# RWKV6 in a hybrid block on one core: layernorm statistics from ScalarE's sums in two passes, the decay's mixed token added by TensorE and multiplied by VectorE

## The chip, the core and the metric

The kernel runs on one core of a Trainium2 chip. A core has five engines, each with its own in-order instruction queue: TensorE (PE; its weight loads are listed as PEld), VectorE (DVE), ScalarE (ACT), GpSimd (POOL) and SyncE (SP), which only issues DMAs. TensorE reads SBUF and writes PSUM; ScalarE and VectorE read both; GpSimd works in SBUF only here. The metric is the device time of one execution in microseconds (us); 0.3% of it is about what can be told from no change.

## The reference

Four layers with residual sums, each on a layernorm of its input: a retention (attention) layer, a mixture of experts (MoE: 8 experts, the best 2 per token), the RWKV6 layer, and the same MoE again. There are 4 sequences of 1024 tokens with 256 channels, all float32.

```python
def _layernorm(x, axis=-1, eps=1e-05):
    m = jnp.mean(x, axis=axis, keepdims=True)
    v = jnp.var(x, axis=axis, keepdims=True)
    return (x - m) / jnp.sqrt(v + eps)
...
x = x + attention(_layernorm(x))
x = x + moe(_layernorm(x))
x = x + rwkv6(_layernorm(x))
x = x + moe(_layernorm(x))
```

What RWKV6 computes, as far as the change touches it:

```python
sx = shifted(x) - x
m = jnp.tanh((x + sx * time_maa_x) @ tm_w1).reshape(Bb, Tt, 5, A)
mix = time_maa_wkvrg + jnp.einsum('btfa,fac->btfc', m, tm_w2)
xw, xk, xv, xr, xg = [x + sx * mix[:, :, i] for i in range(5)]
r, k, v, g = xr @ Wr, xk @ Wk, xv @ Wv, silu(xg @ Wg)
w = jnp.exp(-jnp.exp(time_decay + jnp.tanh(xw @ td_w1) @ td_w2))
# per head, for each token: y = r (state + u k v); state = w state + k v
```

After that y is normalized per head, multiplied by g and by Wo, and added to x. The "decay's mixed token" is xw, the first of the five.

## The kernel before

**Tiling.** The 4096 tokens are eight blocks of 512 (two to a sequence); a block's residual `res[j]` stays in SBUF as 128 tokens x 4 tiles x 256 channels. RWKV works on it transposed: 128 channels by 512 tokens, two channel groups g. The stages follow one another: retention, first MoE, RWKV, second MoE.

**The RWKV stage** is written out by hand. `step(j, n, ...)` (L1272) is step n of block j, eight steps to a block; a step has two halves h. `run(j, n, h)` (L1088) does one part of the recurrence: VectorE multiplies k into the spread-out v (L1094) and runs two scans of 512 tokens (L1096), then GpSimd multiplies by r (L1104). TensorE sums the result into w_yp (L1127). Other work is put between the runs by tables: `given` (L1211) makes the mixed tokens of block j+1, `amid` (L1220) stands in the middle of a step, `late` (L1230) at its end, `uses` (L1240) between the two scans of a run. Through these, block j's recurrence goes on beside the output of block j-1, the projections of block j+1 and the layernorm of block j+2.

**Who decides the order.** TensorE and ScalarE run in program order through the whole kernel, VectorE and GpSimd from the first MoE on, SP in the RWKV stage. What is written later in the program waits behind what is written earlier on the same engine, whether it needs it or not. The products that RWKV makes in PSUM take three banks with the tag "mm" in turn: w_mp, w_dp, w_cp, w_pp, w_yc, w_twp, w_rp and others. A product waits until the bank that was used three products earlier has been read.

**What the change touches.**
- `stats_of` (L201): for each of the four tiles of a block, `bn_stats` and `bn_aggr` on VectorE (L206, L207) give mean and variance; GpSimd forms rstd by `inv_sqrt` (L198, L199) and shift = -mean rstd (L209, L210).
- `normed` of RWKV (L911), at step 5 of block j for block j+2: `stats_of`, then four ScalarE ACTIVATEs that scale and shift (L919), then the token before the block (L923 or L925).
- `Piece.block` (L484) and `Piece.tokens` (L500, by L495): the same for the router of the second MoE, for one finished block n at a time: statistics at the end of step 7 of block n+1, the normalized tokens at the end of step 0 of block n+2, their transposes (`turned`) in step 2, the logits at the end of step 3 (L1543 to L1549).
- `deltas` (L954): a mixed token in two channel groups. TensorE makes w_dp (L964), ScalarE adds `maa` while it reads PSUM (L976), GpSimd multiplies by sx and adds the token (L977, L978). For the tokens 0 and 2 of blocks 6 and 7 one VectorE instruction takes the place of L976 and L977:

```python
                    if f in (0, 2) and j >= NBLK - 2:
                        nc.vector.scalar_tensor_tensor(xf, dp, maa, sx, ALU.add, ALU.mult)
                    else:
                        nc.scalar.activation(xf, dp, AF.Identity, bias=maa)
                        nc.gpsimd.tensor_mul(xf, xf, sx)
                    nc.gpsimd.tensor_add(xf, xf, d["now"][:, c, :])
```

- `decay` (L982), in the middle of step 4 for block j+1: w_twp (L986) is the decay's mixed token times td_w1, and ScalarE's tanh reads it (L989).

**Near them, in one block.** Step 0: `factors(1)` gives the second half of w_wk (L1036, L1037), which `paired` (w_rk, L1019) reads; `mix` makes w_m (L947 to L952), which w_dp needs. Step 1: w_dp of tokens 2 and 0 for the first channel group, `own` (w_cp, L1025), the projection g with Silu (w_gT, L1011, with a table load on ScalarE), `centre` (w_yc, L1140), and the second w_cp; `bonus` (L1030) on VectorE reads w_cp. Step 2: w_dp of tokens 2 and 0 for the second group. Steps 3 and 4: tokens 1 and 3, `root` (L1163 to L1167), `gated` (L1181 to L1183: w_cen, w_sq). Steps 6 and 7: w_op (L225), the projections k and r (L1013), the first half of w_wk for the next block. Block 0 has no block ahead of it: `prepare` (L1268) makes its mixed tokens and its w_twp during the last tiles of the first MoE.

Of the kernel before, what the change touches and what calls it, by code (L numbers as in the profile page):

```python
# [39 lines left out]
F32 = mybir.dt.float32  # L40
I32 = mybir.dt.int32
AF = mybir.ActivationFunctionType
ALU = mybir.AluOpType
AX = mybir.AxisListType

P = 128
B, T, C = 4, 1024, 256
KC = C // P
BLK = 512
NB = T // BLK  # L50
NT = BLK // P
H, D = 16, 16
GH = P // D
E = 8
# [4 lines left out]
NBLK = B * NB  # L59
# [3 lines left out]
HB = NBLK // 2  # L63
HT = HB * NT
# [44 lines left out]
def hybrid_kernel(  # L109
# [24 lines left out]
    nc = tc.nc  # L134
    mm = nc.tensor.matmul
# [3 lines left out]
    def pool(name, side="left"):  # L139
        return tc.alloc_tile_pool(name=name, bufs=1, side=side, reuse_waits="tile")  # L140
# [5 lines left out]
    small = tc.alloc_tile_pool(name="small", bufs=4)  # L146
    ps = banks("ps")

    def psum(shape, name, tag="mm"):

        t = ps.tile([P, 512], F32, name=name, tag=tag, bufs=3 if tag == "mm" else 1)
        n = int(np.prod(shape[1:]))
        if len(shape) == 2:
            return t[:, :n]
        return t[:, :n].rearrange("p (a b) -> p a b", b=shape[2])
# [4 lines left out]
    res = {}  # L160
# [34 lines left out]
    def inv_sqrt(o, var, n, name, scale=1.0):  # L195

        t = small.tile([P, n], F32, name=name, tag=f"var{n}", bufs=2)
        nc.gpsimd.tensor_scalar(t, var, scale, EPS, ALU.mult, ALU.add)  # L198
        nc.gpsimd.tensor_tensor(o, t, mhalf[:, :n], ALU.pow)  # L199

    def stats_of(r, rstd, shift, who):  # L201

        mv = small.tile([P, NT, 2], F32, name=f"{who}mv", tag="mv")
        for i in range(NT):
            st = small.tile([P, 6], F32, name=f"{who}st", tag="st")
            nc.vector.bn_stats(st, r[:, i, :])  # L206
            nc.vector.bn_aggr(mv[:, i, :], st)  # L207
        inv_sqrt(rstd, mv[:, :, 1], NT, f"{who}ve")
        nc.gpsimd.tensor_scalar(shift, mv[:, :, 0], -1.0, None, ALU.mult)  # L209
        nc.gpsimd.tensor_tensor(shift, shift, rstd, ALU.mult)  # L210

    def across(xn, n, out, who):

        tp = psum([P, 2 * KC, P], f"{who}xtp").rearrange("p (i k) t -> p i k t", k=KC)
        for i in range(2):
            for k in range(KC):
                nc.tensor.transpose(tp[:, i, k, :], xn(2 * n + i)[:, k * P : (k + 1) * P], ident)
        nc.scalar.copy(out.rearrange("p k (i t) -> p i k t", i=2), tp)
# [251 lines left out]
    class Piece:  # L470
# [6 lines left out]
        def sm(self, shape, name, dt=F32, bufs=1):  # L477
# [3 lines left out]
            t = t[:, : int(np.prod(shape))]  # L481
            return t if len(shape) == 1 else t.rearrange("p (a b) -> p a b", b=shape[1])

        def block(self, n):  # L484

            if n == 0:
                self.logit = self.sm([HT, E], "m_logit")
                self.rstd = self.sm([HT], "m_rstd", bufs=2)
                self.shift = self.sm([HT], "m_shift", bufs=2)
            cols = slice(n * NT, (n + 1) * NT)  # L490
            stats_of(res[self.start + n], self.rstd[:, cols], self.shift[:, cols], "m_")

        def normed(self, xn, i):

            nc.scalar.activation(  # L495
                xn, res[self.start + i // NT][:, i % NT, :], AF.Identity,
                scale=self.rstd[:, i : i + 1], bias=self.shift[:, i : i + 1],
            )

        def tokens(self, n):  # L500
            xn = self.xn = [ph.tile([P, C], F32, name="m_xn", tag="m_xn", bufs=4) for i in range(NT)]
            for i in range(NT):
                self.normed(xn[i], n * NT + i)

        def turned(self):
            tT = self.tT = ph.tile([P, KC, BLK], F32, name="m_tT", tag="m_tT", bufs=1)
# [389 lines left out]
    def rwkv(pi, w):  # L896
# [3 lines left out]
        st = [dict() for _ in range(NBLK)]  # L900
# [3 lines left out]
        def half(where, name, bufs=2):  # L904
            return where.tile([P, BLK], F32, name=name, tag=name, bufs=bufs)

        def full(where, name, bufs=2, n=BLK):
            return where.tile([P, KC, n], F32, name=name, tag=name, bufs=bufs)


        def normed(j):  # L911
            d = st[j]
            r = res[j]
            rstd = small.tile([P, NT], F32, name="w_rstd", tag="rstd")
            shift = small.tile([P, NT], F32, name="w_shift", tag="shift")
            stats_of(r, rstd, shift, "w_")
            xn = d["xn"] = pi.tile([P, NT, C], F32, name="w_xn", tag="w_xn", bufs=1)
            for i in range(NT):
                nc.scalar.activation(xn[:, i, :], r[:, i, :], AF.Identity,  # L919
                                     scale=rstd[:, i : i + 1], bias=shift[:, i : i + 1])  # L920
            xT = d["xT"] = full(pi, "w_xT", n=BLK + 1)
            if j % NB == 0:
                nc.gpsimd.memset(xT[:, :, 0:1], 0.0)  # L923
            else:
                nc.gpsimd.tensor_copy(xT[:, :, 0:1], st[j - 1]["xT"][:, :, BLK : BLK + 1])  # L925
# [28 lines left out]
        def deltas(j, parts):  # L954


            d = st[j]
            dps = []

            def product(f, c):  # L960
                rows = slice(32 * f, 32 * f + 32) if f < 4 else slice(0, 32)
                wt, m = (w["tm_w2a"], d["m", 0]) if f < 4 else (w["tm_w2b"], d["m", 1])
                dp = psum([P, BLK], "w_dp")
                mm(dp, lhsT=wt[rows, c * P : (c + 1) * P], rhs=m[rows, :], start=True, stop=True)  # L964
                dps.append((f, c, dp))

            def mixed():
                for f, c, dp in dps:
                    if c == 0:
                        d["xf", f] = full(pi, "w_xf", 4)  # L970
                    xf = d["xf", f][:, c, :]
                    maa, sx = vec[:, c, V_MAA + f : V_MAA + f + 1], d["sx"][:, c, :]
                    if f in (0, 2) and j >= NBLK - 2:
                        nc.vector.scalar_tensor_tensor(xf, dp, maa, sx, ALU.add, ALU.mult)
                    else:
                        nc.scalar.activation(xf, dp, AF.Identity, bias=maa)  # L976
                        nc.gpsimd.tensor_mul(xf, xf, sx)  # L977
                    nc.gpsimd.tensor_add(xf, xf, d["now"][:, c, :])  # L978

            return [lambda f=f, c=c: product(f, c) for f, c in parts], mixed  # L980

        def decay(j):  # L982
            d = st[j]
            tp = psum([P, BLK], "w_twp")
            for c in range(KC):
                mm(tp[:64, :], lhsT=w["td_w1"][:, c, :], rhs=d["xf", 0][:, c, :],  # L986
                   start=(c == 0), stop=(c == KC - 1))
            d["tw"] = half(pi, "w_tw", 1)
            nc.scalar.activation(d["tw"][:64, :], tp[:64, :], AF.Tanh)  # L989

# [200 lines left out]
        def both(j, parts):  # L1191
# [4 lines left out]

        first = [
            [(0, normed)],
            [(0, turn)],
            [(0, mix, 0), (0, mix, 1)],  # L1200
            [(0, both, [(0, 0), (0, 1)])],
            [(0, both, [(1, 0), (1, 1)])],
            [(0, both, [(2, 0), (2, 1)]), (0, decay), (1, normed)],
            [(0, both, [(3, 0), (3, 1)])],
            [],
# [17 lines left out]
            2: [(1, mix, 1)],  # L1223
            3: [(1, projected, "v", 2)],
            4: [(-1, spread_out, 0), (1, decay)],
            5: [(1, decay2), (2, normed)],
            6: [(1, projected, "k", 1)],
            7: [(-1, out_part, 2), (1, projected, "r", 3), (1, factors, 0)],
        }
        late = {  # L1230
# [1 line left out]
            1: [(-1, centre, 1), (0, own, 1)],  # L1232
            2: [(-1, spread)],
            3: [],
            4: [(-1, spread_out, 1)],
            5: [(1, store)],
            6: [(-1, out_part, 0)],
            7: [(2, turn), (0, centre, 0)],
# [150 lines left out]
    bias = keep.tile([P, E], F32, name="bias")  # L1389
    nc.sync.dma_start(out=bias, in_=router_b.partition_broadcast(P))  # L1390
    ph = pool("ph")
# [46 lines left out]
    m, mid = moes[0].pieces[:2]  # L1438
# [38 lines left out]
    extra, made = {}, {}  # L1477

    def add(j, f, *a):
        extra.setdefault(j, []).append((f, *a))  # L1480
# [20 lines left out]
    def inputs():  # L1501
        prt.release()
        pi = made["pi"] = pool("pi")
        made["w"] = rwkv_inputs(pi)
        made["rwkv"] = rwkv(pi, made["w"])
# [13 lines left out]
    pi, w = made["pi"], made["w"]  # L1519
# [17 lines left out]
    extra, mids, fronts = {}, {}, {}  # L1537
# [4 lines left out]
        add(SENT[i], next_a.send, i)  # L1542
    for n in range(2 * HB - 1):  # L1543
        m = [p for p in moe.pieces if p.start <= n][-1]
        add(8 * n + 15, m.block, n - m.start)
        add(8 * n + 16, m.tokens, n - m.start)
        fronts[8 * n + 18] = [(m.turned,)]
        add(8 * n + 19, m.product)
        mids[8 * n + 20] = [(m.biased, n - m.start)]  # L1549
# [157 lines left out]
```

## Time and profile before

| | us |
|---|---|
| median of 5 runs | 1609.4 |
| lowest, highest | 1605.38, 1614.41 |
| the profiled execution | 1611.12 |
| its span | 1609.3 |
| busy in the span: PE, PEld | 1359.9, 713.4 |
| busy in the span: DVE, ACT, POOL | 1017.0, 603.6, 924.6 |

The profile is one execution, taken by the hardware profiler, with a span from its first to its last instruction. The page cuts the span into 40 equal slices and gives for each engine the busy share of a slice in tenths (9 is 90% or more). A group is all instructions of one line, operation and shape; behind it stand the busy time, the mean duration of one in ns, and the idle time of the engine just ahead of them with what ended it. In a timeline each line gives start, length, engine, line, operation, output <- inputs and shapes, and in brackets the idle time before it and who ended that. Names such as w_dp are the program's tiles. TensorE's matmuls of float32 data are recorded in parts, so counts on PE are higher than in the program. "Clock" is the share of full speed that TensorE was granted.

The groups that the change counts, in the whole span: L206 and L207 for m_ and w_ together 96 and 96 instructions, L977 72, L978 80, L974 8.

### The profile page before, as it was taken

The numbers are of one execution on the slowest core, as the hardware profiler recorded it, in microseconds if no ns is written. First come the engines' busy times: TensorE is split into PE (matmuls) and PEld (weight loads), VectorE is DVE, ScalarE is ACT, GpSimd is POOL, SyncE is SP. The second block draws the span as 40 slices with busy tenths as digits, with TensorE's granted clock in tenths as the row PEclk, the third lists the DMA queues.
The fourth block names the chain that finished last, engine by engine and source line by source line (L and its number), as shares of the span: only waits on it lengthen the run. The fifth ranks groups of instructions, "written<-read, shape, count | busy, mean of one in ns | idle before, by whom it ended". The sixth has DMA issues, their size and how long they took to land.

```text
span 1609.3 us, 21021 instructions
## 1 busy us (share of the span) xinstructions
PE 1359.9 (84%) x6652; PEld 713.4 (44%) x6652; DVE 1017.0 (63%) x2004; ACT 603.6 (38%) x1436; POOL 924.6 (57%) x881
## 2 busy tenths in 40 slices
PE   5999998868889988987879797887697577889993
PEld 3666665545545644422233232332232234456562
DVE  6566557424433343297988888999989962523444
ACT  2343434333433334434334444443244324333331
POOL 4233323633553326399989898987599844453331
PEclk9999999968889999998879798997789788899997
DMA  8991111131323341256656454534346832232545
GB/s 292 335 316 51 54 54 53 63 114 54 124 93 96 120 130 60 63 143 153 165 128 156 117 141 108 151 101 113 89 126 166 249 124 76 89 106 93 185 131 180
DMA packets 117548, 207.70 MB, mean 129 GB/s; under 512 B 12193, under 2 KB 80001, under 8 KB 117441
## 3 DMA queue, kind: packets, MB, share of 16 engines
q1 hardware_dynamic: 95904, 160.20, 34.5%
q0 software_dynamic: 17184, 39.86, 8.0%
q10 hardware_dynamic: 4352, 6.29, 1.3%
q8 instruction: 57, 0.93, 0.3%
q14 instruction: 51, 0.41, 0.1%
HBM read 139.18 MB, written 67.14 MB: 128 GB/s over the span
## 4 chain that ended last, share of the span: by engine, by line
PE 53%; DVE 17%; POOL 12%; ACT 6%; issue 6%; DMA 4%; another core or an unknown queue 1%; SPq 0%; ACTq 0%; POOLq 0%; DVEq 0%
PE m_hp L788 13%; PE m_op L825 6%; DVE w_s L1096 5%; POOL w_s L1104 5%; PE w_pp L1008 4%; PE a_qkp L291 3%; PE w_yp L1127 2%; PE a_yp L350 2%; DVE w_vb L1094 2%; PE w_dp L964 2%; PE m_lp L520 2%; PE a_sp L330 2%; PE m_xtp L781 2%; PE a_gp L273 2%; PE a_op L225 2%
## 5 line engine op out<-in xcount | busy, mean ns | idle before, releaser
L1104 POOL TENSOR_TENSOR w_s<-w_s,w_rT 128x1024 f32<-128x1024 f32 x128 | 304.1, 2415 | 34.3 <-DVE w_s L1096 30.6
L831 POOL DMA_INDIRECT y_all<-m_y,m_to x142 | 137.3, 967 | 305.0 <-ACT m_xt L783 173.4
L788 PE MATMUL m_hp<-w1a,m_xt 128*128 x568 | 289.1, 634 | 17.4 <-ACT m_xt L783 11.8
L794 DVE TENSOR_TENSOR m_a<-m_hp,m_sg 128x256 f32<-128x256 f32 x142 | 60.1, 424 | 292.7 <-ACT m_sg L792 268.4
L1094 DVE TENSOR_TENSOR w_vb<-w_vb,w_wk 128x1024 f32<-128x1024 f32 x128 | 153.4, 1199 | 28.3 <-ACT w_wk L1037 26.6
L1096 DVE TENSOR_TENSOR_SCAN w_s<-w_wk,w_carry,w_vb 128x512 f32<-128x512 f32 x128 | 161.0, 1276 | 9.3 <-PE w_yp L1127 1.1
L825 PE MATMUL m_op<-w2a,m_aT 128*128 x568 | 152.3, 392 | 13.3 <-ACT m_y L830 7.1
L1096 DVE TENSOR_TENSOR_SCAN w_s<-w_wk,w_vb 128x512 f32<-128x512 f32 x128 | 152.8, 1216 | 15.5 <-ACT w_carry L1114 7.1
L737 POOL DMA_INDIRECT xg_all<-m_row,m_at x128 | 125.5, 980 | 47.6 <-issue 31.3
L788 PEld LDWEIGHTS m_hp<-w1a,m_xt 128*128 128x128 f32 x568 | 103.6, 203 | 94.7 <-issue 80.2
L1127 PE MATMUL w_yp<-w_s,core_c 128*32 128x512 f32 x512 | 100.1, 688 | 44.5 <-POOL w_s L1104 33.2
L792 ACT ACTIVATE m_sg<-m_hp 128x256 f32<-128x256 f32 x142 | 54.5, 384 | 168.3 <-PE m_hp L788 150.8
L830 ACT ACTIVATE m_y<-m_op,m_share 128x256 f32<-128x256 f32 x142 | 67.2, 473 | 128.9 <-PE m_op L825 103.6
L303 POOL TENSOR_TENSOR a_t<-a_t,a_t 128x512 f32<-128x512 f32 x32 | 41.1, 1284 | 123.7 <-DVE a_t L302 104.4
L825 PEld LDWEIGHTS m_op<-w2a,m_aT 128*128 128x128 f32 x568 | 99.4, 195 | 26.1 <-ACT m_y L830 9.0
L977 POOL TENSOR_TENSOR w_xf<-w_xf,w_sx 128x512 f32<-128x512 f32 x72 | 94.1, 1307 | 24.1 <-ACT w_xf L976 23.4
L978 POOL TENSOR_TENSOR w_xf<-w_xf,w_xT 128x512 f32<-128x512 f32 x80 | 87.1, 1090 | 5.6
L333 DVE TENSOR_TENSOR a_pt<-a_sp,ret_c 128x2048 f32<-128x2048 f32 x32 | 73.2, 2286 | 17.4 <-PE a_sp L330 16.8
L818 PEld LDWEIGHTS m_atp<-cst,m_a 128*128 128x128 f32 x284 | 40.5, 146 | 95.7 <-issue 66.8
L291 PE MATMUL a_qkp<-wqkv,a_xT 128*128 128x512 f32 x128 | 68.1, 659 | 0.0
L818 PE MATMUL m_atp<-cst,m_a 128*128 128x128 f32 x284 | 56.0, 280 | 12.4 <-DVE m_a L794 11.5
L783 ACT COPY m_xt<-m_xtp 128x256 f32<-128x256 f32 x142 | 51.8, 365 | 32.5 <-PE m_xtp L781 32.3
(251 smaller groups left out, 2459.9 us busy)
## 6 DMA issues: line engine op xcount, KB each, us to landing
w_vb<-v_all SPq DMA_DIRECT2D x125, 512.0 KB
xg_all<-zero SPq DMA_DIRECT2D x34, 520.0 KB
m_xg<-xg_all SPq DMA_DIRECT2D x34, 520.0 KB
tab<-in_rope SPq DMA_DIRECT2D x32, 512.0 KB
m_back<-y_all SPq DMA_DIRECT2D x48, 256.0 KB
v_all<-w_vT SPq DMA_DIRECT2D x64, 128.0 KB
res<-in_x SPq DMA_DIRECT2D x8, 512.0 KB
w1a<-in_w SPq DMA_DIRECT2D x8, 512.0 KB
```

Of the source, the lines that this page charges most:

```text
L291: mm(qkp, lhsT=xc[:, c, cols], rhs=wqkv[:, c, 0 : 2 * C], start=(c == 0), stop=(c == KC - 1))
L737: nc.gpsimd.indirect_dma_start(out=self.moe.sends[2 * (self.start * NT + i) + n][:, :], out_offset=bass.IndirectOffsetOnAxis(ap=self.at[n] ...
L788: mm(hp, lhsT=self.xt[j][:, c, :], rhs=w1a[:, bass.ds(self.ev[j], 1), c, :].rearrange("p o n -> p (o n)"), start=(c == 0), stop=(c == KC - 1))
L818: nc.tensor.transpose(tp[:, c, :], self.act[j][:, c * P : (c + 1) * P], ident)
L825: mm(op, lhsT=self.aT[j][:, c, :], rhs=w2a[:, bass.ds(self.ev[j], 1), c, :].rearrange("p o n -> p (o n)"), start=(c == 0), stop=(c == KC - 1))
L831: nc.gpsimd.indirect_dma_start(out=self.scatters[j][:, :], out_offset=bass.IndirectOffsetOnAxis(ap=self.to[g][:, i : i + 1], axis=0), in_= ...
L977: nc.gpsimd.tensor_mul(xf, xf, sx)
L978: nc.gpsimd.tensor_add(xf, xf, d["now"][:, c, :])
L1094: nc.vector.tensor_mul(vb, vb, wk[:, 1:2, :].to_broadcast([P, 2, BLK]))
L1096: nc.vector.tensor_tensor_scan(s[:, q, 1 : BLK + 1], wk[:, 0, :], vb[:, q, :], 0.0 if j % NB == 0 else st[j - 1]["carry"][:, n, 2 * h + q ...
L1104: nc.gpsimd.tensor_mul(s[:, :, 0:BLK], s[:, :, 0:BLK], d["r"][:, g, :].unsqueeze(1).to_broadcast([P, 2, BLK]),)
L1127: mm(d["yp", g][32 * q : 32 * q + 32, :], lhsT=w["sel"][:, i, :], rhs=d["s", n, q // 2][:, q % 2, 0:BLK], start=False, stop=(i == 3), skip ...
```

## The change

- The statistics of the layernorm of RWKV for blocks 2 to 7, and of the second MoE's router for blocks 0 to 5, are made by ScalarE in two passes over the four tiles: an Identity that sums (the mean, times -1/C by a small ScalarE operation), and a Square of x - mean that sums. GpSimd still makes rstd and shift. Blocks 0 and 1 of RWKV, and the router's blocks 6 and 7 and all of the first MoE, keep `stats_of`.
- For RWKV the first pass stands at the end of step 4, the second in the middle of step 5, and `normed` moves from step 5 to the middle of step 6.
- For the router the first pass stands at the end of step 7, the second at the end of step 0 of the next block; the tokens move from the end of step 0 to the middle of step 1 (ahead of `own` and the projection g); GpSimd copies rstd and shift into the piece's tiles.
- The decay's mixed token (token 0) is made by the one VectorE instruction in every block, and the token itself isn't added: `decay` multiplies td_w1 with both `now` and the product, so that TensorE adds them in PSUM.

```diff
+    def moments(d, r, n, waste, who):
+        if n == 0:
+            for name in ("mean", "square", "rstd", "shift"):
+                d[name] = small.tile([P, NT], F32, name=f"{who}{name}", tag=f"{who}{name}", bufs=2)
+        for i in range(NT):
+            if n == 0:
+                nc.scalar.activation(waste(i), r[:, i, :], AF.Identity,
+                                     accum_out=d["mean"][:, i : i + 1])
+            else:
+                nc.scalar.activation(waste(i), r[:, i, :], AF.Square, bias=d["mean"][:, i : i + 1],
+                                     accum_out=d["square"][:, i : i + 1])
+        if n == 0:
+            nc.scalar.mul(d["mean"], d["mean"], -1.0 / C)
+        else:
+            inv_sqrt(d["rstd"], d["square"], NT, f"{who}ve", 1.0 / C)
+            nc.gpsimd.tensor_tensor(d["shift"], d["mean"], d["rstd"], ALU.mult)
...
+        def sums(self, n, part):
+            if n == 0 and part == 0:
+                self.block_tiles()
+            if part == 0:
+                self.xn = [ph.tile([P, C], F32, name="m_xn", tag="m_xn", bufs=4) for i in range(NT)]
+                self.sum = {}
+            d = self.sum
+            moments(d, res[self.start + n], part, lambda i: self.xn[i], "m_")
+            if part == 1:
+                cols = slice(n * NT, (n + 1) * NT)
+                nc.gpsimd.tensor_copy(self.rstd[:, cols], d["rstd"])
+                nc.gpsimd.tensor_copy(self.shift[:, cols], d["shift"])
...
+        def sums_of(j, part):
+            d = st[j]
+            if part == 0:
+                d["xn"] = pi.tile([P, NT, C], F32, name="w_xn", tag="w_xn", bufs=1)
+            moments(d, res[j], part, lambda i: d["xn"][:, i, :], "w_")
...
-                    if f in (0, 2) and j >= NBLK - 2:
+                    if f == 0 or f == 2 and j >= NBLK - 2:
                         nc.vector.scalar_tensor_tensor(xf, dp, maa, sx, ALU.add, ALU.mult)
                     else:
                         nc.scalar.activation(xf, dp, AF.Identity, bias=maa)
                         nc.gpsimd.tensor_mul(xf, xf, sx)
-                    nc.gpsimd.tensor_add(xf, xf, d["now"][:, c, :])
+                    if f > 0:
+                        nc.gpsimd.tensor_add(xf, xf, d["now"][:, c, :])
...
-            for c in range(KC):
-                mm(tp[:64, :], lhsT=w["td_w1"][:, c, :], rhs=d["xf", 0][:, c, :],
-                   start=(c == 0), stop=(c == KC - 1))
+            for n, z in enumerate((d["now"], d["xf", 0])):
+                for c in range(KC):
+                    mm(tp[:64, :], lhsT=w["td_w1"][:, c, :], rhs=z[:, c, :],
+                       start=(n + c == 0), stop=(n + c == KC))
...
-            5: [(1, decay2), (2, normed)],
-            6: [(1, projected, "k", 1)],
+            5: [(1, decay2), (2, sums_of, 1)],
+            6: [(2, normed), (1, projected, "k", 1)],
...
-            4: [(-1, spread_out, 1)],
+            4: [(-1, spread_out, 1), (2, sums_of, 0)],
...
-        add(8 * n + 15, m.block, n - m.start)
-        add(8 * n + 16, m.tokens, n - m.start)
+        if n == 2 * HB - 2:
+            add(8 * n + 15, m.block, n - m.start)
+            continue
+        add(8 * n + 15, m.sums, n - m.start, 0)
+        add(8 * n + 16, m.sums, n - m.start, 1)
+        fronts[8 * n + 17] = [(m.tokens, n - m.start, True)]
         fronts[8 * n + 18] = [(m.turned,)]
```

More of the change, by code (lines that the diff above doesn't have):

```diff
@@ L482, in sm, with block_tiles @@
             return t if len(shape) == 1 else t.rearrange("p (a b) -> p a b", b=shape[1])
+        def block_tiles(self):
+            self.logit = self.sm([HT, E], "m_logit")
+            self.rstd = self.sm([HT], "m_rstd", bufs=2)
+            self.shift = self.sm([HT], "m_shift", bufs=2)
         def block(self, n):
             if n == 0:
-                self.logit = self.sm([HT, E], "m_logit")
-                self.rstd = self.sm([HT], "m_rstd", bufs=2)
-                self.shift = self.sm([HT], "m_shift", bufs=2)
+                self.block_tiles()
             cols = slice(n * NT, (n + 1) * NT)
             stats_of(res[self.start + n], self.rstd[:, cols], self.shift[:, cols], "m_")
+        def sums(self, n, part):
+            if n == 0 and part == 0:
+                self.block_tiles()
+            if part == 0:
[7 more added lines that the diff above has]
+                nc.gpsimd.tensor_copy(self.shift[:, cols], d["shift"])
         def normed(self, xn, i):
@@ L498, in normed, with tokens @@
             )
-        def tokens(self, n):
-            xn = self.xn = [ph.tile([P, C], F32, name="m_xn", tag="m_xn", bufs=4) for i in range(NT)]
+        def tokens(self, n, made=False):
+            if not made:
+                self.xn = [ph.tile([P, C], F32, name="m_xn", tag="m_xn", bufs=4) for i in range(NT)]
             for i in range(NT):
-                self.normed(xn[i], n * NT + i)
+                self.normed(self.xn[i], n * NT + i)
         def turned(self):
@@ L913, in normed @@
             r = res[j]
[L914 to L917, printed above, removed]
+            if "xn" not in d:
+                d["rstd"] = small.tile([P, NT], F32, name="w_rstd", tag="w_rstd", bufs=2)
+                d["shift"] = small.tile([P, NT], F32, name="w_shift", tag="w_shift", bufs=2)
+                stats_of(r, d["rstd"], d["shift"], "w_")
+                d["xn"] = pi.tile([P, NT, C], F32, name="w_xn", tag="w_xn", bufs=1)
+            xn, rstd, shift = d["xn"], d["rstd"], d["shift"]
             for i in range(NT):
```

## The prediction

> **What bounds it now.** I read the slices first, then the core by blocks, then one block's timeline engine by engine.
>
> ```profile
> DVE  6566557424433343297988888999989962523444
> ACT  2343434333433334434334444443244324333331
> POOL 4233323633553326399989898987599844453331
> ```
>
> The change lies in slices 17 to 33, the RWKV stage, 681.5 to 1304.8 us: eight blocks j of eight steps n with two halves h. A run (n,h) is a VectorE multiply (L1094, 1.20 us), two scans (1.25 each) and GpSimd's multiply (L1104, 2.35 as a rule). VectorE and GpSimd are both near full, ScalarE is not. By blocks 0, 4 and 5 (columns: window, length, then busy PE, PEld, DVE, ACT, POOL, clock, DMA):
>
> ```profile
> 681.50:753.00 71.50, 57.22 (x165) 17.81 (x163) 59.80 (x60) 25.73 (x53) 66.44 (x60) 0.88 0.61 153
> 981.00:1055.90 74.90, 64.85 (x233) 24.13 (x232) 66.23 (x79) 32.43 (x64) 69.20 (x65) 0.91 0.48 131
> 1055.90:1153.20 97.30, 77.92 (x263) 29.15 (x263) 92.35 (x133) 36.65 (x79) 62.98 (x44) 0.81 0.35 94
> ```
>
> No engine fills block 4, so the period is a chain. Its timeline (last brackets: idle before, and who ended it):
>
> ```profile
> 995.90 2.08 ACT L495 ACTIVATE m_xn<-res,m_shift,m_rstd 128x256 f32<-128x256 f32 x4
> 997.43 0.69 DVE L1030 TENSOR_TENSOR w_bonus<-w_cp,w_vT 128x512 f32<-128x512 f32 x1 [1.88 <-PE w_cp L1025]
> 1000.69 0.60 ACT L1011 ACTIVATE w_gT<-w_pp 128x512 f32<-128x512 f32 x1 [0.26 <-PE w_pp L1008]
> 1003.06 1.12 PE L1025 MATMUL w_cp<-w_rk,w_sum 128*128 128x512 f32 x2
> 1004.22 0.69 DVE L1030 TENSOR_TENSOR w_bonus<-w_cp,w_vT 128x512 f32<-128x512 f32 x1 [2.53 <-PE w_cp L1025]
> 1019.28 2.36 POOL L1104 TENSOR_TENSOR w_s<-w_s,w_rT 128x1024 f32<-128x1024 f32 x1 [1.17 <-DVE w_s L1096]
> 1045.13 1.28 PE L1127 MATMUL w_yp<-w_s,core_c 128*32 128x512 f32 x4 [3.19 <-POOL w_s L1083]
> 1055.91 1.22 DVE L1094 TENSOR_TENSOR w_vb<-w_vb,w_wk 128x1024 f32<-128x1024 f32 x1 [1.39 <-ACT w_wk L1037]
> ```
>
> In steps 0 to 2 VectorE waits for TensorE (second w_cp, 1003.06). From the bonus at 1004.22 it runs on to run (3,1), for which GpSimd waits at 1019.28. From there GpSimd has no gap until run (5,1) ends at 1045.1, for which TensorE waits; w_op, the r projection, ScalarE's w_rT and w_wk lead to the next block at 1055.9, and TensorE goes on to the next w_cp. Blocks 2 and 3 have the same waits (1.70 and 2.53, 1.51 and 2.38; at run (3,1) 0.52 and 1.52). In blocks 0 and 1 GpSimd has no wait from 686 to 825; block 5 is VectorE's, with the routing in it.
>
> **The change by parts.** Rows for the prices (busy, mean ns):
>
> ```profile
> L206 DVE BATCH_NORM_STATS2 w_st<-res 128x6 f32<-128x256 f32 x24 | 9.5, 397 | 0.0
> L207 DVE BATCH_NORM_AGGREGATE w_mv<-w_st 128x2 f32<-128x6 f32 x24 | 4.4, 182 | 0.8
> L974 DVE SCALAR_TENSOR_TENSOR w_xf<-w_dp,vec,w_sx 128x512 f32<-128x512 f32 x8 | 5.6, 740 | 2.4 <-PE w_dp L964 2.4
> L977 POOL TENSOR_TENSOR w_xf<-w_xf,w_sx 128x512 f32<-128x512 f32 x64 | 83.9, 1310 | 23.6 <-ACT w_xf L976 23.2 <-ACT w_s L1086 0.4
> L978 POOL TENSOR_TENSOR w_xf<-w_xf,w_xT 128x512 f32<-128x512 f32 x72 | 78.3, 1089 | 5.0
> ```
>
> Statistics: twelve groups of four tiles leave VectorE, each 4 x (0.397 + 0.182) = 2.3 us; six belong to w_ (step 5 of blocks 0 to 5), six to m_ (end of blocks 1 to 6). Mixed token: GpSimd loses 16 adds of 1.09 and 12 multiplies of 1.31, so 4.8 us in each of blocks 0 to 4 and 2.2 in 5 and 6; VectorE gains 2 x 0.74 in blocks 0 to 4; ScalarE loses two 0.68 evacuations there; TensorE doubles w_twp, 1.9 us at full clock, 3.6 in block 5 at a granted 0.55. VectorE's balance in the stage: -0.8, then four times -3.1, -4.6, -2.3, 0: -20.1 us.
>
> ScalarE gains 96 ACTIVATEs that also sum. None like that is in the trace. From below, the nearest rows are 128x256 ACTIVATEs of the MoE stage with no column operand (L792, 384 ns) and with one (L830, 473 ns); from above, the same and behind each one a small COPY (w_carry L1114, 192 ns) that would read the sum. Four cost 1.5 to 2.3 us for the means, 1.9 to 2.7 for the squares. I take 2.1 for either, nearer the bare rows, because four with two column operands take 2.08 together at 995.90; 0.2 more is the small operation that scales the means.
>
> Prologue, before 681: TensorE is full there (16.16 of 17 us from 650 to 667), so block 0's longer w_twp costs **+1.9**.
>
> Block 0: GpSimd is 7.6 us behind VectorE at run (3,1) (719.7 against 712.1), so its 4.8 come off whole, and VectorE's 1.5 more leave it ahead: **-4.8**. The wait of 6.04 on s buffers at 744.3 shrinks with it.
>
> Block 1: GpSimd is only 1.4 us behind at run (3,1) (788.46 against 787.05). Relieved, it waits there for VectorE, which comes 1.5 later: **+0.1**. The 4.8 are lost.
>
> Blocks 2 to 4, told on block 4. The means go ahead of w_wk of the second half on ScalarE: ready at 992.7 in place of 990.4, and w_rk (991.29) waits 1.5. The first new L974 waits for w_dp, done at 996.3, so that is hidden; its 0.74 takes the place of the 1.88 wait; the bonus comes at 999.5, before 1004.1, and is late for nobody. The squares stand where m_xn stood, to 998.0. GpSimd, done with runs (0,0) and (0,1) at 993.8, now waits for them, with run (1,0) and a mix queued behind; it catches up by run (2,1), having 4.8 us less to do. (Should it not, TensorE's w_yp of step 1 would wait: 1 us per us.) Its chain (0.19 + 1.04 + 0.20 and two copies like L925, 0.19 each, with gaps) ends at 1000.0. Only then m_xn runs on ScalarE, with the Silu table load (1.28) and w_gT queued behind: w_gT 0 ends at 1004.0 instead of 1001.3. The second w_cp needs the PSUM bank that w_gT 0 was read from (three "mm" banks in turn): 1004.1 instead of 1003.06, **+1.05**. Behind it TensorE has two w_yp groups (1.04 each) ahead of the w_dp that the second new L974 reads: that is done at 1008.2, L974 at 1008.9, and run (2,1) starts there instead of at 1005.95: +2.95. A wait of 0.39 at 1016.03 goes, GpSimd's shift loses one step of 0.23: **+2.3** at run (5,1). A second path agrees: w_twp longer by 2.6 makes w_tw, and w_cen behind it on ScalarE, end at 1031.4; w_sq on GpSimd needs that and ran at 1028.86. The statistics taken from VectorE lie under GpSimd's gapless stretch (w_) and under the w_wk wait (m_): worth nothing here. No DMA is added or moved, and SP's queue keeps its order. Three blocks: **+6.9**.
>
> Block 5: VectorE's own. -2.3 at step 5; of the 2.3 at its end some 0.8, since w_wk is due 13.3 us after run (5,1) and VectorE would be there after 12.0; the later w_cp and the pair of L974 behind it cost 1.5: **-1.6**. Block 6 (its closing wait of 1.74 hides its 2.3) has the late w_cp: **+1.7**. Block 7 has no deltas, but the late w_gT: **+1.0**.
>
> Sum: 1.9 - 4.8 + 0.1 + 6.9 - 1.6 + 1.7 + 1.0 = +5.2 us on the profiled execution (1611.12, span 1609.3): 1616.3. The median of the runs is 1.7 lower: **1614.6, say 1615**. About 0.3% (4.8 us) can be told from no change.
>
> The trace has a tile's statistics at 0.58 us on VectorE and, by the rows, 0.86 on ScalarE. The Trainium skill (ScalarE: Activation LUTs, Rules for kernel authors) says that adds and multiplies belong on VectorE; by it the move costs 48 x 0.28 = 13 us of engine time, by the windows (30 of 78 us busy in a block) ScalarE has that time and only its order costs. The trace has w_twp at 1.93 us with clock 1.00 and 3.60 with 0.55. The Trainium skill (TensorE: Matmul & The Clock Gate, Part 1) says that the clock halves after an idle window; by it more matmuls could win back clock, which would make the added w_twp 1.9 everywhere, not 2.6.
>
> **Rivals.** *The relief pays* (33%): if slack that I don't see hides the late w_cp and L974, VectorE's balance counts whole: 1611.1 + 1.9 - 20.1 - 1.7 = 1591; with GpSimd's 28 us as the floor 1583. For it: 93% busy. Against it: gaps of 6.4 us in block 4 that end on TensorE and ScalarE. *ScalarE's detour binds whole* (14%): squares, chain and m_xn in a row cost 4.0, of which I count 1.05 because w_gT had 1.8 us of slack and the lost evacuation 0.7. If sums are at their upper price, or GpSimd reaches the chain one multiply late (2.35), each us goes through: +3.0 in six blocks, 1633. It decides from w_gT 0 ending later than 1003. *Gains and losses cancel* (10%): blocks 2 to 4 lose only L974's 0.74 each: 1610. The change does do what it says: the order of instructions in the changed kernel has these counts.
>
> **Numbers.** Forecast 43%, by itself 1603 to 1624 (sums at their bounds, the second path in all blocks): 0.02 of it under 1604.6, 0.13 from there to 1614.2, 0.28 above. Faster: 0.33 + 0.02 = 0.35. Within: 0.10 + 0.13 = 0.23. Slower: 0.28 + 0.14 = 0.42. The range, 1584 to 1632, takes in the first rival to its floor and leaves out half of the second.
>
> **What would show it.** Block 0 shorter by about 5 us; blocks 2 to 4 about 77 to 80 long; w_gT 0 some 2.7 us later after w_yc than now; VectorE's idle before L1094 at block ends up from 1.4 to some 5; GpSimd idle before the m_ chain, ended by ScalarE. Wrong, if blocks 2 to 4 get shorter or if an accumulating ACTIVATE costs over 0.7.

## The result and the profile after

The change costs 0.3%: 1616.2 us (median of 52 runs) against 1611.7 (94 runs of the kernel before beside them), ratio 1.0031, 95% interval 1.0020 to 1.0041. The profiled execution took 1605.05 (span 1603.1), below the median of its own kernel. Its prologue (672.2 instead of 681.5 us) and the stages behind RWKV are shorter than in the profile of before, but the starts of the stage in all profiles below lie anywhere from 664 to 687. So the RWKV stage is compared, which holds the change.

The slices of the page of after:

```profile
DVE  6666666435523443398978797889978872523544
ACT  2343434433333333544454545363343424333331
POOL 4233322725453334499998887876679854453331
```

The change did what it says: in the stage VectorE's digits fell from 9 and 8 to 8 and 7, GpSimd's too, ScalarE's rose. The stage by windows (after; length, then busy PE, PEld, DVE, ACT, POOL), blocks 0, 4, 5, 6:

```profile
672.17:739.37 67.20, 56.72 (x169) 17.77 (x167) 59.27 (x55) 28.37 (x68) 62.34 (x55) 0.90 0.67 164
967.07:1046.17 79.10, 68.04 (x237) 26.12 (x236) 63.91 (x65) 38.69 (x97) 64.02 (x60) 0.89 0.44 120
1046.17:1140.57 94.40, 75.05 (x263) 27.49 (x263) 88.00 (x117) 42.85 (x112) 58.84 (x41) 0.86 0.35 95
1140.57:1223.47 82.90, 64.99 (x216) 23.96 (x214) 65.18 (x68) 30.68 (x77) 69.62 (x64) 0.86 0.51 136
```

VectorE's work in the stage fell by 20.3 us (561.8 to 541.5, predicted 20.1), and its idle time rose by 27.4 (61.5 to 88.9): the stage is 7.1 longer, 630.4 against 623.3. All blocks, against the prediction's terms (a block differs by up to 3 us between profiles of kernels that are alike in it):

| block | 0 | 1 | 2 | 3 | 4 | 5 | 6 | 7 |
|---|---|---|---|---|---|---|---|---|
| before | 71.5 | 73.6 | 78.4 | 76.0 | 74.9 | 97.3 | 74.5 | 77.1 |
| after | 67.2 | 71.4 | 79.2 | 77.1 | 79.1 | 94.4 | 82.9 | 79.1 |
| difference | -4.3 | -2.2 | +0.8 | +1.1 | +4.2 | -2.9 | +8.4 | +2.0 |
| predicted | -4.8 | +0.1 | +2.3 | +2.3 | +2.3 | -1.6 | +1.7 | +1.0 |

Block 4 of after, in order of time (timeline; in brackets the idle time before, and who ended it):

```profile
978.69 0.69 DVE L1067 TENSOR_TENSOR w_rk<-w_wk,w_rT 128x512 f32<-128x512 f32 x1 [1.27 <-ACT w_wk L1085]
983.16 0.19 POOL L198 TENSOR_SCALAR m_ve<-m_square 128x4 f32<-128x4 f32 x1 [3.15 <-ACT m_xn L223]
985.02 2.07 ACT L531 ACTIVATE m_xn<-res,m_shift,m_rstd 128x256 f32<-128x256 f32 x4 [1.38 <-POOL m_shift L527]
988.41 1.08 ACT L1059 ACTIVATE w_gT<-w_pp 128x512 f32<-128x512 f32 x2
989.06 1.12 PE L1188 MATMUL w_yc<-w_y,tail_c 128*128 128x512 f32 x2 [1.60 <-ACT w_gT L1059]
994.03 0.75 DVE L1019 SCALAR_TENSOR_TENSOR w_xf<-w_dp,vec,w_sx 128x512 f32<-128x512 f32 x1 [1.13 <-PE w_dp L1009]
1018.07 0.59 ACT L1037 ACTIVATE w_tw<-w_twp 64x512 f32<-64x512 f32 x1 [9.86 <-PE w_twp L1034]
1019.44 1.28 POOL L1231 TENSOR_TENSOR w_sq<-w_cen,w_gT 128x512 f32<-128x512 f32 x1 [2.36 <-ACT w_cen L1230]
1020.18 0.69 DVE L1229 TENSOR_TENSOR w_cen<-w_cen,w_rp 128x512 f32<-128x512 f32 x1 [2.52 <-PE w_rp L1222]
1046.24 1.22 DVE L1142 TENSOR_TENSOR w_vb<-w_vb,w_wk 128x1024 f32<-128x1024 f32 x1 [4.30 <-ACT w_wk L1085]
```

This is the predicted chain: w_rk waits for the means, GpSimd for the squares, ScalarE's m_xn for GpSimd, w_gT and TensorE stand behind m_xn, and VectorE's second L1019 (L974 of before) waits for w_dp. Below stand two waits at `decay`: GpSimd's w_sq behind ScalarE's w_tw, which the prediction has, and VectorE's w_cen for the second w_rp, which it does not have. Counted from the start of the block, run (2,1) begins 2.6 us later than in before (27.6 against 24.9) and GpSimd's part of run (3,1) 2.1 later (40.3 against 38.3). The second w_cen comes 4.7 later (53.0 against 48.4): the chain brings some 2 us here, the wait for w_rp the rest. Block 6 of after:

```profile
1146.39 0.50 ACT L223 ACTIVATE m_xn<-res,m_mean 128x256 f32<-128x256 f32 x1
1146.79 0.19 ACT L223 ACTIVATION_READ_ACCUMULATOR m_xn<-res,m_mean 128x1 f32 x1
1159.84 0.19 POOL L198 TENSOR_SCALAR m_ve<-m_square 128x4 f32<-128x4 f32 x1
1161.72 2.07 ACT L531 ACTIVATE m_xn<-res,m_shift,m_rstd 128x256 f32<-128x256 f32 x4 [13.75 <-POOL m_shift L527]
1165.11 1.08 ACT L1059 ACTIVATE w_gT<-w_pp 128x512 f32<-128x512 f32 x2
1165.76 1.84 PE L1073 MATMUL w_cp<-w_rk,w_sum 128*128 128x512 f32 x2 [4.97 <-ACT w_gT L1059]
1167.64 0.69 DVE L1078 TENSOR_TENSOR w_bonus<-w_cp,w_vT 128x512 f32<-128x512 f32 x1 [7.25 <-PE w_cp L1073]
```

The squares were done at 1148.0, but in this block GpSimd has four scatters of the second MoE (L774, which send tokens) and two multiplies ahead of m_ve: from 1150.1 to 1159.8. They are ahead of it because m_ve is now written with the second pass, at the end of step 0. ScalarE stands at m_xn for 13.75 us with w_gT, whose projection ended by 1160, behind it, and VectorE waits 7.25. In block 6 of before, where the statistics came from VectorE, m_ve stood ahead of the third scatter, and m_xn was done before TensorE had the projection:

```profile
1163.10 0.19 POOL L198 TENSOR_SCALAR m_ve<-m_mv 128x4 f32<-128x4 f32 x1
1164.96 2.08 ACT L495 ACTIVATE m_xn<-res,m_shift,m_rstd 128x256 f32<-128x256 f32 x4 [8.34 <-POOL m_shift L210]
1169.72 0.60 ACT L1011 ACTIVATE w_gT<-w_pp 128x512 f32<-128x512 f32 x1 [1.38 <-PE w_pp L1008]
```

### The profile page after: what moved, and what is told of

Read it like the earlier page. It is cut to its first block, busy times and chain, and to the rows that moved or that the text cites. A ratio compares the mean times of both kernels' runs of the same rounds, so it can differ in the third digit from the quotient of the medians.

```text
span 1603.1 us, 21167 instructions
## 1 busy us (share of the span) xinstructions
PE 1356.9 (85%) x6684; PEld 712.4 (44%) x6684; DVE 997.4 (62%) x1920; ACT 640.2 (40%) x1628; POOL 891.4 (56%) x853
## 4 chain that ended last, share of the span: by engine, by line
PE 53%; DVE 20%; POOL 10%; ACT 7%; issue 5%; DMA 4%; another core or an unknown queue 1%; SPq 0%; DVEq 0%; POOLq 0%; ACTq 0%
PE m_hp L825 12%; PE m_op L862 6%; DVE w_s L1144 6%; POOL w_s L1152 3%; DVE w_vb L1142 3%; PE a_qkp L310 3%; PE w_pp L1056 3%; PE w_dp L1009 2%; PE a_yp L369 2%; PE m_lp L557 2%; PE w_yp L1175 2%; ACT m_xn L531 2%; PE a_sp L349 2%; PE a_op L244 2%; PE w_twp L1034 2%
## 5 line engine op out<-in xcount | busy, mean ns | idle before, releaser
L1142 DVE TENSOR_TENSOR w_vb<-w_vb,w_wk 128x1024 f32<-128x1024 f32 x128 | 153.6, 1200 | 43.9 <-ACT w_wk L1085 43.2
L774 POOL DMA_INDIRECT xg_all<-m_row,m_at x128 | 125.5, 980 | 50.6 <-issue 30.2
L1175 PE MATMUL w_yp<-w_s,core_c 128*32 128x512 f32 x512 | 93.8, 666 | 32.5 <-POOL w_s L1152 24.2
L867 ACT ACTIVATE m_y<-m_op,m_share 128x256 f32<-128x256 f32 x142 | 67.2, 473 | 130.0 <-PE m_op L862 103.2
L1022 POOL TENSOR_TENSOR w_xf<-w_xf,w_sx 128x512 f32<-128x512 f32 x60 | 77.3, 1289 | 23.0 <-ACT w_xf L1021 22.8
L1025 POOL TENSOR_TENSOR w_xf<-w_xf,w_xT 128x512 f32<-128x512 f32 x64 | 69.8, 1090 | 5.0 <-DVE w_xf L1019 0.3
L310 PE MATMUL a_qkp<-wqkv,a_xT 128*128 128x512 f32 x128 | 63.9, 623 | 0.0
```

Of the source, the lines that this page charges most:

```text
L310: mm(qkp, lhsT=xc[:, c, cols], rhs=wqkv[:, c, 0 : 2 * C], start=(c == 0), stop=(c == KC - 1))
L774: nc.gpsimd.indirect_dma_start(out=self.moe.sends[2 * (self.start * NT + i) + n][:, :], out_offset=bass.IndirectOffsetOnAxis(ap=self.at[n] ...
L1142: nc.vector.tensor_mul(vb, vb, wk[:, 1:2, :].to_broadcast([P, 2, BLK]))
L1175: mm(d["yp", g][32 * q : 32 * q + 32, :], lhsT=w["sel"][:, i, :], rhs=d["s", n, q // 2][:, q % 2, 0:BLK], start=False, stop=(i == 3), skip ...
```

## The experiments

Theory **Q** puts the loss on ScalarE's queue (w_gT behind an m_xn that waits for GpSimd), theory **D** on the decay's part. The runs were timed in three groups, e1 to e4, e5 to e8, e9 to e12, each on one chip beside its own runs of the kernel before (medians 1600.8, 1616.6, 1603.8). Ratios of one group compare closely, those of different groups less so. The length of the stage, of its blocks 2 to 4 and of its blocks 6 and 7, VectorE's idle time and ScalarE's busy time in the stage are from the one profile of each, in us.

| run | ratio [95%] | stage | blocks 2 to 4 | blocks 6, 7 | VectorE idle | ScalarE |
|---|---|---|---|---|---|---|
| before | 1 | 623.3 | 229.3 | 151.6 | 61.5 | 242 |
| after | 1.0031 [1.0020, 1.0041] | 630.4 | 235.4 | 162.0 | 88.9 | 280 |
| e1 statistics alone | 1.0020 [0.9992, 1.0048] | 628.7 | 228.0 | 159.9 | 94.1 | 286 |
| e2 decay's part alone | 1.0055 [1.0031, 1.0079] | 634.3 | 239.1 | 154.2 | 66.7 | 237 |
| e3 two m_ groups back | 1.0018 [0.9988, 1.0048] | 626.4 | 236.6 | 154.3 | 77.6 | 274 |
| e4 tokens late | 0.9991 [0.9976, 1.0007] | 622.7 | 236.8 | 154.4 | 78.0 | 282 |
| e5 e1, tokens late | 0.9977 [0.9956, 0.9998] | 616.5 | 227.9 | 152.4 | 78.3 | 287 |
| e6 e2, decay moved | 0.9893 [0.9863, 0.9922] | 606.4 | 220.8 | 151.3 | 38.6 | 239 |
| e7 e4, decay moved | 0.9817 [0.9790, 0.9844] | 596.9 | 216.5 | 150.5 | 52.4 | 282 |
| e8 before, decay moved | 0.9899 [0.9874, 0.9924] | 608.4 | 218.1 | 150.4 | 47.4 | 244 |
| e9 after, decay moved | 0.9935 [0.9910, 0.9960] | 618.7 | 225.6 | 162.3 | 78.4 | 282 |
| e10 e5, decay moved | 0.9889 [0.9860, 0.9919] | 609.6 | 221.0 | 152.1 | 71.9 | 288 |
| e11 e7, decay ahead of w_rp | 0.9865 [0.9839, 0.9891] | 606.7 | 225.0 | 152.9 | 62.9 | 282 |
| e12 e7, all m_ on VectorE | 0.9831 [0.9807, 0.9856] | 604.7 | 224.7 | 150.7 | 49.2 | 260 |

**e1, the statistics alone**: `deltas` and `decay` as before.

```diff
-                    if f == 0 or f == 2 and j >= NBLK - 2:
+                    if f in (0, 2) and j >= NBLK - 2:
...
```

> The changed kernel with the decay's mixed token as before: only the statistics are changed. Theory Q (the queue: ScalarE's m_xn waits for GpSimd's m_shift, the Silu load and w_gT stand behind it, and the second w_cp waits for the bank of w_gT): slower than before by 8 to 12 us, and the waits of VectorE on w_cp in blocks 6 and 7 (7.25 and 6.08 us in the changed kernel) stay. Theory D (the decay's L974 and the longer w_twp are what costs): same as before or up to 4 us faster.

1605.8 us, ratio 1.0020 with an interval that reaches 1: between the two. Its blocks 6 and 7 have the waits of after (7.48 and 6.06 at w_bonus) and are 81.0 and 78.9 long; no w_cen waits over 0.9.

**e2, the decay's part alone**: the statistics as before.

> The kernel before with only the decay's mixed token changed (VectorE makes the product, TensorE adds). Theory Q: 2 to 6 us faster than before, with block 0 shorter by 4 to 5 us and no wait of over 3 us on w_cp. Theory D: slower than before by 4 us or more. The prediction's own terms for this part come to +2 (prologue +1.9, block 0 -4.8, three blocks +1.6 each).

1609.1 us: theory D. No block has a w_bonus wait over 1.5, but w_cen waits twice, 4.0 in all, in each of blocks 2, 4 and 6. VectorE also waits for w_dp at L974, 16.0 in the stage instead of 2.4, but as the prediction has it this takes the place of waits at w_bonus, which fall from 14.4 to 4.6; the 12.1 at w_cen (0.6 before) come on top. Block 4 of e2:

```profile
1014.71 3.68 PE L989 MATMUL w_twp<-w_xT,w_td_w 128*64 128x512 f32 x4
1018.17 2.13 PE L989 MATMUL w_twp<-w_xf,w_td_w 128*64 128x512 f32 x4
1022.46 0.69 DVE L1184 TENSOR_TENSOR w_cen<-w_cen,w_rp 128x512 f32<-128x512 f32 x1 [3.26 <-PE w_rp L1177]
```

**e3, the router's groups of blocks 4 and 5 back on VectorE.**

```diff
+        if n < HB:
+            add(8 * n + 15, m.sums, n - m.start, 0)
...
+        else:
+            add(8 * n + 15, m.block, n - m.start)
+            add(8 * n + 16, m.tokens, n - m.start)
```

> The changed kernel, but the router's statistics of blocks 4 and 5, whose tokens fall into blocks 6 and 7 of the recurrence, stay on VectorE as before. Theory Q: 8 to 11 us below the changed kernel (ratio to before 0.996 to 0.998), blocks 6 and 7 at 74 to 78 us again. Theory D: as the changed kernel (ratio 1.003).

1605.3 us: the time misses Q's 0.996 to 0.998, and its interval is too wide to tell it from after. In its profile blocks 6 and 7, the ones it alters, are 78.2 and 76.2 instead of 82.9 and 79.1, and their w_bonus waits are gone, as Q has it.

**e4, m.tokens behind everything of its step** instead of ahead of `own` and the projection g.

```diff
-        fronts[8 * n + 17] = [(m.tokens, n - m.start, True)]
+        add(8 * n + 17, m.tokens, n - m.start, True)
```

> The changed kernel with the router's four m_xn ACTIVATEs moved from the middle of step 1 to its end, so that w_gT and w_yc are ahead of them on ScalarE; nothing else. Theory Q: 8 to 14 us below the changed kernel (ratio to before 0.994 to 0.998), no wait of VectorE on w_cp over 3 us in blocks 6 and 7, and w_gT no more behind m_shift. Theory D: as the changed kernel.

1599.3 us, 0.4% below the change, which is less than Q's 8 to 14 us: Q, for this part of the loss. Blocks 6 and 7 fall by 7.6 in all and have no wait at w_bonus; blocks 2 to 4 stay as long as in after. ScalarE's work is what it was (282 us).

**e5, e1 with e4's edit.**

> Both layernorms' statistics from ScalarE's sums as in the change, the mixed token as before, and m.tokens queued behind everything of its step instead of ahead of the run, so that the w_gT of the same step no longer stands behind it on ScalarE. Queue theory (the loss of the statistics alone is ScalarE waiting at m_xn for GpSimd's m_shift with w_gT behind it, and nothing else): w_cp's wait for w_gT in blocks 6 and 7 goes, the time falls 3 to 8 us below the statistics alone, ratio to the kernel before 0.995 to 0.999. Rival (the loss is the 37 us more of ScalarE's work, wherever it stands): the time stays with the statistics alone, ratio 1.000 to 1.004.

0.9977, with an interval that just leaves out 1: once w_gT no longer stands behind m_xn, the statistics no longer cost time, and the rival, ScalarE's amount of work, falls (287 us). The profile says it more clearly: blocks 6 and 7 are 7.5 shorter than in e1, and blocks 2 to 4 are the same.

**e6, e2 with the whole of decay behind the second w_rp**, one run later; **e8, the kernel before with that alone.**

```diff
-            4: [(-1, spread_out, 0), (1, decay)],
+            4: [(-1, spread_out, 0)],
...
-            4: [(-1, spread_out, 1)],
+            4: [(-1, spread_out, 1), (1, decay)],
```

> The kernel before with the decay's part of the change alone, and the whole of decay put from behind the first w_rp (spread_out 0) to behind the second one (spread_out 1), one run later. Theory W (the loss of the decay's part is the second w_rp standing on TensorE behind the doubled w_twp, with w_cen on VectorE waiting for it): the waits of 2 to 3.3 us in blocks 2, 4 and 6 go, 3 x 3 = 9 us come back, ratio 0.998 to 1.001 instead of 1.0055. Theory C (the loss is the second multiply, L974 in the kernel before's lines, in VectorE's chain): nothing comes back, ratio 1.004 to 1.007. Rival: decay one run later makes w_dp and w_xf late for the block after, slower than 1.007.

> The kernel before with decay put behind the second w_rp and nothing else: the control for the two runs before this. With a w_twp that is not doubled there is little to wait for: ratio 0.998 to 1.002. If it is faster by more than 0.3%, the place of decay was worth something in the kernel before too, and that much of the gain of the other two is not the doubled w_twp's.

Against e2, e6 gives back 1.6% instead of the 0.6 of theory W; theory C falls, L974 is still there. But e8, the control, gives 1.0% by itself against its expectation. What the decay's part costs therefore hangs on the place: +0.55% in the old one, and in the new one nothing (0.9893 against 0.9899). Block 4 of e6 has w_rp ahead and a short wait (the first w_cen's wait rose to 2.20, so the waits of blocks 2, 4 and 6 fell from 12.1 to 5.6, not to none):

```profile
1012.87 2.08 PE L1177 MATMUL w_rp<-w_rstd,tail_c 128*128 128x512 f32 x2
1014.87 3.37 PE L989 MATMUL w_twp<-w_xT,w_td_w 128*64 128x512 f32 x4
1014.98 0.69 DVE L1184 TENSOR_TENSOR w_cen<-w_cen,w_rp 128x512 f32<-128x512 f32 x1 [0.47 <-PE w_rp L1177]
```

In block 4 of e8 ScalarE does the first w_cen well ahead of w_tw:

```profile
1019.57 0.81 ACT L1182 ACTIVATE w_cen<-w_cen,w_ln 128x512 f32<-128x512 f32 x1 [5.78 <-DVE w_cen L1181]
1026.03 0.59 ACT L989 ACTIVATE w_tw<-w_twp 64x512 f32<-64x512 f32 x1 [3.64 <-PE w_twp L986]
```

In before w_tw waited 6.49 for w_twp, to 1026.51, with w_cen behind it. The 4.0 us by which e8's block 4 is shorter are idle time of VectorE: its two waits at w_bonus fall from 1.88 and 2.53 to none and 1.51, and the 1.39 ahead of the next block's L1094 is gone.

**e7, both orders altered.**

> The change with both orders altered: m.tokens behind everything of its step, and decay behind the second w_rp. Queue theory and theory W together: below the change with m.tokens late alone (0.9991) by the 3 waits of 2 to 3 us, ratio 0.993 to 0.997. If only the queue costs: 0.998 to 1.000. If decay one run later costs more than it frees: above 1.001.

1588.3 us, 1.8% below the kernel before, lower than expected. VectorE's idle time falls to 52.4. In block 6 GpSimd's m_shift is as late as in after, but w_gT is ahead of it:

```profile
1148.26 0.60 ACT L1059 ACTIVATE w_gT<-w_pp 128x512 f32<-128x512 f32 x1 [7.19 <-PE w_pp L1056]
1152.87 2.08 ACT L531 ACTIVATE m_xn<-res,m_shift,m_rstd 128x256 f32<-128x256 f32 x4 [0.63 <-POOL m_shift L527]
```

**e9, decay moved and m.tokens where the change has it.**

> The change with decay behind the second w_rp, and m.tokens ahead of the run, where the change has it. Queue theory (m.tokens ahead of the run costs wherever decay stands, by w_gT behind m_xn in blocks 6 and 7): 0.4 to 0.6% above the run with both orders altered (0.9817), so 0.985 to 0.989, and w_bonus waits of over 4 us for w_cp in blocks 6 and 7. Rival (with decay one run later GpSimd has m_shift ready in time, and the place of m.tokens no longer matters): 0.980 to 0.983.

0.9935: Q with a larger price than expected, 1.2% above e7 (stage 21.8 longer). Block 6 has the 7.49 wait at w_bonus again, block 7 one of 6.07.

**e10, e5 with decay moved: e7 without the mixed token's part.**

> The statistics with m.tokens late and decay behind the second w_rp, without the change's mixed token. If the parts add up (statistics with late tokens 0.9977, decay moved 0.9899): 0.987 to 0.989, and the mixed token's part is worth 0.5% in the run with both orders altered (0.9817). If the mixed token's part is worth nothing once decay is moved (0.9893 against 0.9899): 0.980 to 0.984.

0.9889: the parts add up. Against e8 (0.9899) the statistics by themselves are then worth nothing that can be told, and neither was the mixed token's part in e6 (0.9893); both together, in e7, are worth 0.8%. Why they need each other isn't shown. It may be that with ScalarE's sums in the chain that runs through GpSimd, GpSimd's relief counts: e10 has waits of VectorE for w_op (3.73 in block 2, 2.51 in block 4) that e7 has not.

**e11, decay one run later but ahead of the second w_rp** (the edit as it stands against e7).

```diff
-            4: [(-1, spread_out, 1), (1, decay), (2, sums_of, 0)],
+            4: [(1, decay), (-1, spread_out, 1), (2, sums_of, 0)],
```

> As the run with both orders altered, but decay, one run later, stands ahead of the second w_rp instead of behind it: the two swap places on TensorE and nothing else moves. Theory W (what costs is the second w_rp behind the doubled w_twp): w_cen on VectorE waits 2 us or more for w_rp in blocks 2, 3 and 4 again, ratio 0.988 to 1.000. Rival (what pays is decay being one run later, with ScalarE's w_tw no longer ahead of what the next block needs): 0.980 to 0.984.

0.9865, between the two. The wait of theory W is back, larger than ever, in blocks 2, 3, 4 and 6 (4.95 to 5.38; block 4 of e11):

```profile
1011.05 1.12 PE L1222 MATMUL w_rp<-w_rstd,tail_c 128*128 128x512 f32 x2
1012.21 0.69 DVE L1229 TENSOR_TENSOR w_cen<-w_cen,w_rp 128x512 f32<-128x512 f32 x1 [5.06 <-PE w_rp L1222]
```

Yet its VectorE idles only 10.5 us more than e7's, because e7's waits for w_wk ahead of L1142, 2.9 to 3.8 at the start of blocks 2 to 5 and 7, are gone: VectorE comes later, and w_wk is ready. So w_rp behind w_twp is the smaller part; most of what moving gives (0.9991 in e4, 0.9865 here, 0.9817 in e7) comes from decay being one run later. Which of decay's instructions pays for that, w_tw on ScalarE or w_twp on TensorE, these runs don't separate.

**e12, e7 with all of the router's statistics on VectorE** (and its tokens where before has them).

> The change with decay behind the second w_rp and all of the second layernorm's statistics (m) back on VectorE as in the kernel before; the first layernorm's (w) stay on ScalarE. If the first layernorm's statistics and the mixed token bring the gain, and the second's only cost ScalarE's time: at or below the run with both orders altered, 0.979 to 0.983. If both layernorms bring their share (VectorE's 2.3 us of each in every block): 0.984 to 0.988.

0.9831, not to be told from e7, and its interval touches both expectations: inconclusive between them. In its own group it is the fastest (1576.4 us against 1584.3 to 1594.4), though in the profiles its stage is 7.8 longer than e7's. No gain in time from the router's six groups on ScalarE is seen.

**Where the loss lies.** The two columns of blocks put it in two places. Blocks 6 and 7 are 10.4 longer in after than in before, 8.3 with the statistics alone (e1) and 2.6 with decay's part alone (e2); with m.tokens late (e4, e5) most of this goes. That is the queue. Blocks 2 to 4 are 6.1 longer in after, 9.8 with decay's part alone, and not longer with the statistics alone (-1.3); the place of m.tokens changes nothing there (e4 against after, e5 against e1). So there it is decay's part that costs, though the queue's chain stands in them too: without it VectorE only waits longer at w_cen (12.1 us in the stage of e4, 8.9 in that of after). Once decay is moved, the chain does cost there (e9 against e7, 9.1).

## Why the prediction was right, and where its steps were not

The forecast (0.3% slower, the order of ScalarE's queue eating what VectorE and GpSimd win) held in sign and size, and the queue's order does cost time. But most of that cost was predicted in blocks 2 to 4 (+6.9, against +2.7 in blocks 6 and 7), and there, the runs show, decay's part is what binds; the queue's cost is in blocks 6 and 7 (+10.4 in all, 8.3 with the statistics alone). That the size came out is partly luck: block 6 cost 6.7 us more than its term, blocks 0, 1 and 5 together 3.1 less than theirs. Step by step:

- *Balance of VectorE, -20.1 in the stage.* Measured -20.3, and the match is luck: 3.7 of it are two instructions of the routing in block 7 that the change doesn't touch (m_eq, 3.07 and 2.19 us in before, 0.22 and 1.34 in after). Blocks 0 to 6 lost 16.6. None of it reached the end: idle time rose by more.
- *Prologue, +1.9.* No run shows this term: the stage starts at 681.5, 674.3 and 686.7 in before, e1 and e8, which are alike up to there.
- *Price of a sum, 2.1 for four.* Squares 2.07 (pitch 0.49), means 1.6 (pitch 0.40). The limit of 0.7 for "wrong" was far off. The Trainium skill (ScalarE activation tables: per-element evaluation and per-set limits, What a function is on this engine) says that the accumulator output adds up the results along the free dimension, and gives no price; the trace shows a second instruction of 0.19 for it, which lies mostly under the next ACTIVATE.
- *Block 0, -4.8; block 1, +0.1.* -4.3 as argued: block 0 is 66.0 to 68.3 in all profiles with the mixed token's part and 71.5 to 73.7 in those without. -2.2 in block 1, which was not forecast; it is 71.8 in e1 and 72.9 in e2, so both parts may have a share.
- *Blocks 2 to 4, +6.9.* +6.1 in all (0.8, 1.1 and 4.2), but e1 and e4 show that the chain isn't what these blocks wait for last. It stands in block 4 as written: w_rk's 1.5 (1.27), GpSimd idle ahead of m_ve (3.15), the second w_cp late by w_gT (predicted 1.05, measured 0.8), run (2,1) late by w_dp (predicted 2.95, measured 2.6), VectorE idle at the block ends "from 1.4 to some 5" (4.2 to 4.6 ahead of blocks 2 to 5). One sign was half: w_gT 0 ended 14.4 after ScalarE's first read of w_yc in the block, before 13.1; 1.3 later, not 2.7. The stretch from the squares to the end of w_gT 0 grew by 2.6, as forecast (8.0, against 5.4 from m_xn in before), but TensorE took 1.2 less from w_yc to w_mp, for which ScalarE waits ahead of it. (In the rivals, 4.0 less 1.8 and 0.7 would be 1.5, not 1.05; the 1.05 comes from the times of the chain.)
- *The second path by w_tw.* w_sq did wait 2.36 for ScalarE. That it "agrees" with the first, and so costs nothing more, was the step that failed in kind: e2, with no sums at all, loses 0.55%, and blocks 2, 4 and 6 wait there for the second w_rp, which the prediction doesn't name. The added TensorE time was sized rightly: 4 x 0.852 us for w_twp in before, 4 x (0.896 + 0.603) after, +2.6.
- *Block 6, +1.7.* +8.4, with a wait of 2.14 for w_rp in it: the step that was mis-sized most. "GpSimd reaches the chain one multiply late" was priced in the rival; in block 6 it is late by two scatters and two multiplies, since m_ve moved behind them in GpSimd's order. The rival's condition (w_gT late, then each us goes through) held there, not in six blocks; in block 7 VectorE waits 6.08 at the same place, but the block is only 2.0 longer.
- *Block 5, -1.6; block 7, +1.0.* -2.9 and +2.0, within what profiles differ.
- *The relief pays* (rival, 1591) did not happen here, but its amount was there: e7 is the change with two orders altered and takes 28 us off the kernel before, 11.6 off e8, which has the moved decay alone.

On the clock the prediction weighed that more matmuls could win it back. In e2's block 4 the first four of w_twp took 0.92 each, the last four 0.53. The granted clock there was 0.50 from 1008.5 to 1018.6, with TensorE busy all the time (10.10 us), and 1.00 on both sides; in the 3.4 us ahead of it TensorE was idle for 1.25. The Trainium skill (TensorE: Matmul & The Clock Gate, Part 1) has half rate after an idle window of about 3.4 us and the full one after some 3.4 us of work; this stretch began after less idle time and lasted longer than that. The four at the end were the cheaper ones, but all eight stood ahead of w_rp.

## What to carry to other kernels

Before work goes to an engine with free time, look at what stands behind it in that engine's queue: an instruction that waits for a third engine holds everything behind it, and the engine's busy share (39% of the stage before) does not show that. A relief of the fullest engines pays only after the next wait in line is moved: the same edit cost 0.3% and, with two pieces of work put elsewhere in the order, was worth 0.8% over the kernel before with decay in the same place. Try the new order on the kernel before as well; more than half of the best version's gain (1.0 of 1.8%) was in the order alone. And read a loss by blocks before naming its cause: here one wait cost time in blocks 6 and 7, and another in blocks 2 to 4.

## What was not expected of the hardware

An ACTIVATE that also sums is two instructions in the trace, 0.41 (Identity) or 0.50 us (Square with a column operand) for 128x256, and ACTIVATION_READ_ACCUMULATOR, 0.19; the next ACTIVATE starts 0.09 us after the read does, so one costs 0.40 or 0.49. A doubled accumulation group on TensorE that starts on a slow clock paid 3.5 us for its first half and 2.1 for its second (block 4 of e2, granted clock 0.50, then 1.00).
